# Recurrence states of four batches on the 128 partitions of a decoder layer

## The chip, the cores and the metric

The kernel runs on one core of a Trainium2 chip. The metric is the device time of one execution in microseconds. The times shown are medians of several executions; the profile is one further execution, recorded by the hardware profiler.

A core has a matrix engine (TensorE, PE in the profile, with its weight loads listed apart as PEld), a vector engine (VectorE, DVE), an engine for activation functions (ScalarE, ACT), a general engine (GpSimd, POOL) and one that issues most DMA transfers (SyncE, SP). [...]

## The reference

One decoder layer on 16 batches of 256 tokens with 256 features, all in float32. Three blocks follow each other, each with a residual and a layer normalization without gain. The change concerns the first, a gated linear recurrence:

```python
h  = x @ in_w.T + in_b                       # 256 -> 512 features
hc = conv(h, conv_w) + conv_b                # causal, 4 taps, by feature
h  = silu(hc)
xp = h @ xp_w.T + xp_b                       # 512 -> 32
a  = exp(-exp(xp[..., :16]))
b  = silu(xp[..., 16:]) * sum(h, axis=-1)
state = state * a_t + b_t                    # scan over the 256 tokens, 16 states a batch
out = states @ out_w.T + out_b               # 16 -> 256
x = layernorm(x + out)
```

The second block is an attention with 8 heads of width 128, whose queries come from x and whose keys and values come from x and from 77 context tokens. The third routes each token to two of eight experts with a limited number of places.

## The kernel before

The kernel has three stages, one after the other.

**Start** (to about 76 us). The weights are loaded on SP's queue in the order of the program. The recurrence of batches 0 and 1 is computed, and the context tokens are normalized and turned into keys' input (`kvc`) and values (`pvc`, L365).

**Loop over heads** (about 76 to 1080 us). 16 batches times 8 heads, 128 steps. Every step has on PE the products for keys and queries of its head (`pk`, `pq`), the output product of the head two steps back (`po`), the scores (`s`), and the transposes of the last head's probabilities (`pa`, `pb`). Everything else is hung into these steps: a table `steps[b, h]` lists what is issued in head h of batch b, right behind `pk` and `pq` of that head (function `at`). So while batch b runs through its heads, the next batch's recurrence and values are prepared, and the last batch's output projection (`pw`), routing and dispatch are finished.

**Experts** (from about 1080 us). The rows that were scattered to `xg` are read back, multiplied and written out.

The recurrence is done for a pair of batches, 512 tokens (`PB = 2`, `PT = 512`):

- `rec_in(pr, c)`, for each of four chunks c of 128 features: the input product `ph`, a copy with bias on ACT, the four taps on DVE, tanh on ACT, and the product that makes silu on DVE. The result is `hs`, 128 features by 4 chunks by 512 tokens, with one buffer.
- `rec_state(pr)`: the product of `hs` with `xpw`, four matmuls with 80 columns into one PSUM bank. Rows 0 to 15 of the bank are the first half of xp, rows 32 to 47 the second half, and rows 64 to 79 the sum over h (those columns of `xpw` are constants). On 16 partitions follow two exponentials and a tanh (ACT), three products (DVE) and two scans of 256 tokens (DVE), into `ysT`, whose 17th row is one and stands for the bias.
- `rec_out(b)`, for one batch: two matmuls with 17 rows (`py`), the sum with the token rows `xt`, the layer normalization, and the load of `xt` two batches on.

In the loop, for the pair that begins with batch nb = b + 1: `rec_in` in heads 4 to 7 of batch b - 1, `rec_state` in head 0 of batch b, `rec_out(nb)` in head 1, `prep_norm(nb)` in head 2, `rec_out(nb + 1)` and `prep_keys(nb)` in head 3.

PSUM tiles made by `bank()` without a tag share two banks: `px`, `py`, `ph`, `pv`, `pw`, `pt` and the router's products take turns there.

Within these lists a scheduler that builds the program may move an instruction past others on its engine; the order is fixed when the kernel is built.

Of the kernel before, what the change touches and what calls it, by code (L numbers as in the profile page):

```python
# [18 lines left out]
P = 128  # L19
B, S, D = 16, 256, 256  # L20
# [5 lines left out]
NST = 16  # L26
# [12 lines left out]
def decoder_layer(  # L39
# [44 lines left out]
    def bank(name, tag="mm", bufs=2):  # L84
        return ps.tile([P, 512], F32, tag=tag, bufs=bufs, name=name)
# [10 lines left out]
    ident = cpool.tile([P, P], F32, tag="ident", name="ident")  # L96
# [33 lines left out]
    def rsqrt(v, n, rows, name):  # L130
        r = small.tile([P, n], F32, tag="r", name=f"r{name}")
        G.tensor_tensor(r[:rows], v[:rows], nhalf[:rows, 0:n], ALU.pow)
        return r

    def layernorm(dst, src, n, rows, name):

        mv = small.tile([P, n, 2], F32, tag="mv", name=f"mv{name}")
        for i in range(n):
            st = small.tile([P, 6], F32, tag="st", name=f"st{name}_{i}")
            V.bn_stats(st[:rows], src[:rows, i, :])  # L140
            V.bn_aggr(mv[:rows, i, :], st[:rows])
        v = small.tile([P, n], F32, tag="v", name=f"v{name}")
        V.tensor_scalar(v[:rows], mv[:rows, :, 1], EPS, None, ALU.add)
        r = rsqrt(v, n, rows, name)
        for i in range(n):
            V.tensor_scalar(
                dst[:rows, i, 0:D], src[:rows, i, :], mv[:rows, i, 0:1], r[:rows, i : i + 1], ALU.subtract, ALU.mult
            )
        return mv, r
# [17 lines left out]
    aw = rec.enter_context(tc.tile_pool(name="aw", bufs=1, side="right"))  # L167
    a2 = rec.enter_context(tc.tile_pool(name="a2", bufs=2, side="right"))
# [15 lines left out]
    b2 = work.enter_context(tc.tile_pool(name="b2", bufs=2))  # L184
    b1 = work.enter_context(tc.tile_pool(name="b1", bufs=1))

    xTs, xts = {}, {}
# [6 lines left out]
    def load_x(b):  # L194
        xts[b] = aw.tile([P, 2, D], F32, tag="xt", bufs=3, name=f"xt{b}")
        nc.sync.dma_start(xts[b], x_in[b * S : (b + 1) * S, :].rearrange("(i p) d -> p i d", p=P))
# [16 lines left out]
    for t0, t1 in ((0, 1), (1, 5), (5, NCT - 1), (NCT - 1, NCT)):  # L213
        c = b2.tile([P, t1 - t0, D], F32, tag="v" if t1 - t0 == 4 else "ctx", name=f"ctx{t0}")
        rows = ctx_rows(t0)
# [2 lines left out]
        )  # L218
        ctxs += [c[:, i, :] for i in range(t1 - t0)]

    xpw = aw.tile([P, NI, 80], F32, tag="xpw", name="xpw")
    G.memset(xpw, 0.0)
    G.memset(xpw[:, :, 64:80], 0.5)
    xpw_d = xp_wT.rearrange("(c p) s -> p c s", p=P)
    nc.sync.dma_start(xpw[:, :, 0:NST], xpw_d[:, :, 0:NST])
    nc.sync.dma_start(xpw[:, :, 32 : 32 + NST], xpw_d[:, :, NST : 2 * NST])
    xpb = aw.tile([64, 1], F32, tag="xpb", name="xpb")
    G.memset(xpb, 0.0)
    nc.sync.dma_start(xpb[0:NST], xp_b[0:NST])
    nc.sync.dma_start(xpb[32 : 32 + NST], xp_b[NST : 2 * NST])  # L230
    outw = aw.tile([NST + 1, D], F32, tag="outw", name="outw")
    nc.sync.dma_start(outw[0:NST], out_wT)
    nc.sync.dma_start(outw[NST : NST + 1], out_b)
    wkv_d = wkv.rearrange("(c p) f -> p c f", p=P)
    nc.sync.dma_start(wkv_s[:, :, INNER:], wkv_d[:, :, INNER:])
    load_x(0)
# [5 lines left out]

    V.tensor_scalar(cw, cw, 0.5, None, ALU.mult)
    V.tensor_scalar(cb, cb, 0.5, None, ALU.mult)
    xpbh = aw.tile([64, 1], F32, tag="xpbh", name="xpbh")
    V.tensor_scalar(xpbh, xpb, 0.5, None, ALU.mult)

    bqs = wpool.tile([P, H], F32, tag="bqs", name="bqs")
    V.tensor_scalar(bqs, bq_s, DH**-0.5, None, ALU.mult)
# [20 lines left out]
        nc.sync.dma_start(w2_s[e], w2T[e].rearrange("(c p) d -> p c d", p=P))  # L270


    hss, yss, xs, stats = {}, {}, {}, {}

    def rec_in(pr, c):

        if c == 0:
            hss[pr] = aw.tile([P, NI, PT], F32, tag="hs", name=f"hs{pr}")
        ph = bank(f"ph{pr}_{c}")
        for k in range(DC):  # L280
            T.matmul(ph, lhsT=inw[:, k, c * P : (c + 1) * P], rhs=xTs[pr][:, k, :], start=(k == 0), stop=(k == DC - 1))  # L281
        hp = a2.tile([P, PB, KC - 1 + S], F32, tag="hp", name=f"hp{pr}_{c}")
        G.memset(hp[:, :, 0 : KC - 1], 0.0)
        A.activation(
            hp[:, :, KC - 1 :], ph.rearrange("p (b s) -> p b s", b=PB), AF.Identity, bias=inb[:, c : c + 1]
        )
        cv = a2.tile([P, PB, S], F32, tag="cv", name=f"cv{pr}_{c}")
        V.tensor_scalar(cv, hp[:, :, 0:S], cw[:, c, 0:1], cb[:, c : c + 1], ALU.mult, ALU.add)
        for k in range(1, KC):
            V.scalar_tensor_tensor(cv, hp[:, :, k : k + S], cw[:, c, k : k + 1], cv, ALU.mult, ALU.add)  # L290
        z = cv.rearrange("p b s -> p (b s)")
        th = a2.tile([P, PT], F32, tag="th", name=f"th{pr}_{c}")
        A.activation(th, z, AF.Tanh)
        V.scalar_tensor_tensor(hss[pr][:, c, :], th, 1.0, z, ALU.add, ALU.mult)

    def rec_state(pr):

        hs = hss.pop(pr)
        px = bank(f"px{pr}")
        for c in range(NI):  # L300
            T.matmul(px[0:80], lhsT=xpw[:, c, :], rhs=hs[:, c, :], start=(c == 0), stop=(c == NI - 1))  # L301
        dec = aw.tile([NST, PT], F32, tag="dec", name=f"dec{pr}")
        A.activation(dec, px[0:NST], AF.Exp, bias=xpb[0:NST])
        A.activation(dec, dec, AF.Exp, scale=-1.0)
        bs = aw.tile([NST, PT], F32, tag="bs", name=f"bs{pr}")
        A.activation(bs, px[32 : 32 + NST], AF.Tanh, bias=xpbh[32 : 32 + NST], scale=0.5)
        zb = aw.tile([NST, PT], F32, tag="zb", name=f"zb{pr}")
        V.tensor_scalar(zb, px[32 : 32 + NST], xpb[32 : 32 + NST], None, ALU.add)
        V.scalar_tensor_tensor(bs, bs, 1.0, zb, ALU.add, ALU.mult)
        V.tensor_tensor(bs, bs, px[64 : 64 + NST], ALU.mult)  # L310

        ysT = a2.tile([NST + 1, PT], F32, tag="ysT", name=f"ysT{pr}")
        G.memset(ysT, 1.0)
        for i in range(PB):
            cols = slice(i * S, (i + 1) * S)
            V.tensor_tensor_scan(ysT[0:NST, cols], dec[:, cols], bs[:, cols], 0.0, ALU.mult, ALU.add)
        yss[pr] = ysT

    def rec_out(b):

        pr, i = divmod(b, PB)
        py = bank(f"py{b}")
        for h in range(2):
            c0 = i * S + h * P
            T.matmul(py[:, h * D : (h + 1) * D], lhsT=yss[pr][:, c0 : c0 + P], rhs=outw, start=True, stop=True)
        y = b2.tile([P, 2, D], F32, tag="ya", name=f"ya{b}")
        V.tensor_tensor(
            y.rearrange("p h d -> p (h d)"),
            py,
            xts.pop(b).rearrange("p h d -> p (h d)"),  # L330
            ALU.add,
        )
        xs[b] = xpool.tile([P, 2, DX], F32, tag="xs", name=f"xs{b}")
        stats[b] = layernorm(xs[b], y, 2, P, f"a{b}")
        if b + 2 < B:
            load_x(b + 2)


    JCS = [(0, P), (P, P), (2 * P, M)]
# [322 lines left out]
    def at(b, h, f, *args):  # L662
        if 0 <= b < B:
            steps[b, h].append((f, args))
# [4 lines left out]
    for b in range(B):  # L669
        nb = b + 1  # L670
        new_pair = nb % PB == 0 and nb < B
        if b > 0:
            early = int(b == B - 1)
            at(b, 2, project, b - 1, 0)
            at(b, 3, project, b - 1, 1)
            at(b, 5 - early, turn_tokens, b - 1)
            at(b, 6 - early, score_experts, b - 1)
            at(b, 6 - early, choose, b - 1)
            at(b, 7 - early, dispatch, b - 1)
            at(b, 7, settle, b - 1)  # L680
        if new_pair:
            at(b, 0, rec_state, nb // PB)
            at(b, 1, rec_out, nb)
            at(b, 2, prep_norm, nb)
            at(b, 3, rec_out, nb + 1)
            at(b, 3, prep_keys, nb)
            for n, h in enumerate((4, 5, 6, 7)):
                at(b, h, prep_values, nb, n)
        elif nb < B:
            at(b, 0, prep_norm, nb)  # L690
            at(b, 0, prep_keys, nb)
            for n, h in enumerate((1, 4, 5, 6)):
                at(b, h, prep_values, nb, n)
            if nb + 1 < B:
                pr = (nb + 1) // PB
                at(b, 0, load_xT, pr)
                for c in range(NI):
                    at(b, 4 + c, rec_in, pr, c)

    rec_in(0, 0)  # L700
    rec_in(0, 1)
# [1 line left out]
    rec_in(0, 2)  # L703
    rec_in(0, 3)
    context(1)
    rec_state(0)
    context(2)
    context(3)
    rec_out(0)
    prep_norm(0)  # L710
    prep_keys(0)
# [21 lines left out]
    rows, xets = {}, {}  # L733
# [171 lines left out]
    for e in range(LAST + 1):  # L905
# [4 lines left out]
        y = second_product(e, it)  # L910
# [55 lines left out]
```

## Time and profile before

| what | us |
|---|---|
| median of 3 runs | 1229.26 (1229.24 to 1230.31) |
| profiled execution, its own time | 1232.08 |
| span of the profiled execution | 1230.4 |
| stage to 76 us: PE busy | 60.13 |
| 76 to 1080 us: PE busy | 995.96 of 1004 |
| 1080 to 1230 us: PE busy | 131.21 of 150 |
| px (L301): PE busy | 29.1 |
| py (L325): PE busy | 18.0 |

The mean granted clock of PE is 0.988 of full speed. A row of the profile names an engine, a line, an operation, the tile written and the tiles read, and the shape in partitions by elements. "Idle before" is the time in which the engine did nothing ahead of these instructions, and behind the arrow stands what ended it. A matmul's busy time contains time in which the next matmul already runs; so sums of busy time on PE are larger than what the matmuls take in a row.

### The profile page before, as it was taken

The numbers are of one execution on the slowest core, as the hardware profiler recorded it, in microseconds if no ns is written. First come the engines' busy times: TensorE is split into PE (matmuls) and PEld (weight loads), VectorE is DVE, ScalarE is ACT, GpSimd is POOL, SyncE is SP. The second block draws the span as 40 slices with busy tenths as digits, with TensorE's granted clock in tenths as the row PEclk, the third lists the DMA queues.
The fourth block names the chain that finished last, engine by engine and source line by source line (L and its number), as shares of the span: only waits on it lengthen the run. The fifth ranks groups of instructions, "written<-read, shape, count | busy, mean of one in ns | idle before, by whom it ended". The sixth has DMA issues, their size and how long they took to land.

```text
span 1230.4 us, 15284 instructions
## 1 busy us (share of the span) xinstructions
PE 1187.3 (96%) x5000; PEld 842.3 (68%) x5000; DVE 725.9 (59%) x2122; ACT 489.4 (40%) x1270; POOL 274.5 (22%) x500
## 2 busy tenths in 40 slices
PE   7799999999999999999999999999999999889995
PEld 3356777767776777677767776777677778756663
DVE  6535755684558555756486548564766464555654
ACT  3135434443435344534353434443543344313331
POOL 3200021122111311131111210221021112135566
PEclk9899999999999999999999999999999999999998
DMA  8730100010001100010000000000001000146762
GB/s 262 245 107 1 37 18 29 9 54 18 29 9 32 37 11 20 26 37 5 19 21 28 12 19 19 22 9 14 9 13 43 13 9 3 29 146 147 177 158 82
DMA packets 43617, 60.80 MB, mean 49 GB/s; under 512 B 7945, under 2 KB 31414, under 8 KB 43538
## 3 DMA queue, kind: packets, MB, share of 16 engines
q1 hardware_dynamic: 36674, 50.34, 12.8%
q0 software_dynamic: 6144, 9.48, 3.3%
q8 instruction: 39, 0.64, 0.2%
q14 instruction: 40, 0.33, 0.1%
q10 hardware_dynamic: 720, 0.01, 0.0%
HBM read 36.55 MB, written 30.78 MB: 55 GB/s over the span
## 4 chain that ended last, share of the span: by engine, by line
PE 82%; DVE 7%; POOL 3%; issue 3%; DMA 3%; ACT 1%; POOLq 0%; SPq 0%; DVEq 0%
PE po L484 12%; PE pk L433 10%; PE s L448 10%; PE pw L502 9%; PE pq L438 8%; PE pv L413 8%; PE ph L281 5%; PE pa L471 4%; PE pi L798 3%; PE pvc L365 3%; PE px L301 2%; PE pf L814 2%; PE pb L471 2%; PE pl L544 1%; DMA xe<-xg 1%
## 5 line engine op out<-in xcount | busy, mean ns | idle before, releaser
L450 DVE TENSOR_REDUCE nm<-s 128x2 f32<-128x666 f32 x128 | 108.4, 847 | 144.7 <-PE s L448 144.4
L484 PE MATMUL po<-ptt,v 128*128 128x256 f32 (+1 forms) x768 | 190.2, 382 | 2.2 <-DVE ptt L473 2.2
L484 PEld LDWEIGHTS po<-ptt,v 128*128 128x128 f32 (+1 forms) x768 | 144.2, 191 | 57.1 <-issue 32.7
L433 PE MATMUL pk<-kvt,wkv_s 128*128 128x333 f32 x512 | 165.1, 444 | 0.0
L448 PE MATMUL s<-kt,qt 128*128 128x333 f32 x512 | 164.4, 442 | 0.0
L492 ACT ACTIVATE ot<-po,bkv_s 128x256 f32<-128x256 f32 x128 | 60.6, 474 | 235.4 <-PE po L484 235.3
L454 ACT ACTIVATE p<-s,nm 128x333 f32<-128x333 f32 x256 | 135.1, 534 | 37.9 <-DVE nm L450 28.6
L438 PE MATMUL pq<-kvt,wq_s 128*128 128x256 f32 x512 | 131.2, 379 | 0.0
L413 PE MATMUL pv<-wkv_s,kvt 128*128 128x512 f32 x256 | 121.6, 599 | 0.0
L448 PEld LDWEIGHTS s<-kt,qt 128*128 128x128 f32 x512 | 96.5, 189 | 31.2 <-ACT qt L440 0.5
L438 PEld LDWEIGHTS pq<-kvt,wq_s 128*128 128x128 f32 x512 | 96.7, 189 | 30.5 <-issue 0.5
L474 ACT COPY ptt<-pb 77x256 f32<-77x256 f32 x128 | 47.1, 368 | 177.3 <-PE pb L471 175.9
L502 PE MATMUL pw<-wo_s,ot 128*128 128x256 f32 x512 | 117.2, 381 | 0.0
L502 PEld LDWEIGHTS pw<-wo_s,ot 128*128 128x128 f32 x512 | 97.4, 191 | 13.4 <-ACT ot L492 0.2
L433 PEld LDWEIGHTS pk<-kvt,wkv_s 128*128 128x128 f32 x512 | 87.6, 191 | 23.0
L459 DVE TENSOR_SCALAR pn<-p,rs 128x333 f32<-128x333 f32 x256 | 93.1, 397 | 4.2
L471 PEld LDWEIGHTS pa<-ident,pn 128*128 128x128 f32 x512 | 63.5, 141 | 38.7 <-DVE pn L459 11.1
L649 POOL DMA_INDIRECT xg<-xs,sidx x64 | 67.3, 1052 | 93.1 <-DVE sidx L646 78.4
L473 DVE COPY ptt<-pa 128x512 f32<-128x512 f32 x128 | 87.3, 682 | 0.9 <-PE pa L471 0.6
L513 POOL TENSOR_TENSOR xb<-xs,bo_s 128x256 f32<-128x256 f32 x32 | 21.2, 684 | 283.4 <-DVE yb L515 283.4
L471 PE MATMUL pa<-ident,pn 128*128 128x128 f32 x512 | 78.8, 274 | 5.9 <-DVE pn L459 5.9
L290 DVE SCALAR_TENSOR_TENSOR cv<-hp,cw,cv 128x512 f32<-128x512 f32 x96 | 71.4, 749 | 2.0
(167 smaller groups left out, 1596.4 us busy)
## 6 DMA issues: line engine op xcount, KB each, us to landing
v<-vc SPq DMA_DIRECT2D x16, 308.0 KB
vc<-vc SPq DMA_DIRECT2D x9, 512.0 KB
xg<-zero SPq DMA_DIRECT2D x17, 262.0 KB
xe<-xg SPq DMA_DIRECT2D x8, 524.0 KB
xT<-in_xT SPq DMA_DIRECT2D x8, 512.0 KB
xt<-in_x_in SPq DMA_DIRECT2D x16, 256.0 KB
out<-o SPq DMA_DIRECT2D x16, 256.0 KB
w<-in_w1T SPq DMA_DIRECT2D x8, 512.0 KB
```

The source lines that it names most:

```text
L290: V.scalar_tensor_tensor(cv, hp[:, :, k : k + S], cw[:, c, k : k + 1], cv, ALU.mult, ALU.add)
L413: T.matmul(pv, lhsT=kvts[b][:, k, jc * P : (jc + 1) * P], rhs=wkv_s[:, k, INNER + f0 : INNER + f0 + 512], start=(k == 0), stop=(k == DC - 1),)
L433: T.matmul(pk[:, 0:J], lhsT=wkv_s[:, k, f], rhs=kvt[:, k, :], start=(k == 0), stop=(k == DC - 1))
L438: T.matmul(pq[:, 0:S], lhsT=wq_s[:, k, f], rhs=kvt[:, k, 0:S], start=(k == 0), stop=(k == DC - 1))
L448: T.matmul(s[:, ic, 0:J], lhsT=qt[:, ic * P : (ic + 1) * P], rhs=kt, start=True, stop=True)
L450: V.tensor_reduce(nm, s[:, :, 0:J], AX.X, ALU.max, negate=True)
L454: A.activation(p[:, ic, :], s[:, ic, 0:J], AF.Exp, bias=nm[:, ic : ic + 1], accum_out=sm[:, ic : ic + 1])
L459: V.tensor_scalar(pn[:, ic, :], p[:, ic, :], rs[:, ic : ic + 1], None, ALU.mult)
L471: T.transpose(dst[0:jn, c0 : c0 + P], pn[:, ic, j0 : j0 + jn], ident)
L473: V.tensor_copy(ptt[:, 0:2, :], pt01.rearrange("p (j i) -> p j i", j=2))
L484: T.matmul(po[:, 0:S], lhsT=vs[b][0:jn, jc, h * DH : (h + 1) * DH], rhs=ptt[0:jn, jc, :], start=(jc == 0), stop=(jc == 2),)
L502: T.matmul(pws[b][:, i * D : (i + 1) * D], lhsT=ot[:, h, i * P : (i + 1) * P], rhs=wo_s[:, h, :], start=(h == 0), stop=(h == H - 1),)
```

## The change

The states of four batches lie side by side on the partitions, 32 partitions to a batch: 16 for the first half of xp, 16 for the second.

- `rec_in` adds up the four chunks of `hs` into `sums` on POOL, three additions of 128x512 for each pair. `hs` and `sums` have two buffers.
- `rec_state(first, last)` works on a group of batches: 0 and 1, 2 and 3, then 4 to 7, 8 to 11, 12 to 15. For each of four batches and each chunk there is one matmul with 32 columns and 256 tokens, which writes to the batch's 32 partitions of one bank (a column tile). Where a group has two batches, the four places hold them twice. Four more matmuls (`sg`) multiply `sums` with a constant 0.5 and so put the sum over h on all partitions. A matmul with a permutation (`perm`, 128x128) brings the second half of xp onto the partitions of the first. Exponentials, tanh, products and one scan then run on 128 partitions by 256 tokens, and `one_row` adds one to the row of each batch that stands for the bias.
- `rec_add(b)` makes the output products of two batches in turn; each has 32 rows, on partitions of its own (a row tile), and a bank of its own. It also adds `xt` and loads the next two `xt`. `rec_out(b)` keeps only the layer normalization.
- `outw` and `xpb` are loaded four times, once for each 32 partitions.
- `rec_in` of the second pair of a group comes in heads 4 to 7 of batch nb - 2, that of the first pair in heads 1, 3, 5 and 7 of batch nb - 3, where nb is the group's first batch. `rec_add` is in head 1 of every batch before a pair.

```diff
-    xpw = aw.tile([P, NI, 80], F32, tag="xpw", name="xpw")
-    G.memset(xpw, 0.0)
-    G.memset(xpw[:, :, 64:80], 0.5)
...
+    xpw = aw.tile([P, NI, 2 * NST], F32, tag="xpw", name="xpw")
+    nc.sync.dma_start(xpw, xp_wT.rearrange("(c p) s -> p c s", p=P))
+    half = aw.tile([P, 2 * NST], F32, tag="half", name="half")
+    G.memset(half, 0.5)
+    xpb = aw.tile([P, 1], F32, tag="xpb", name="xpb")
+
+    outw = aw.tile([P, D], F32, tag="outw", name="outw")
+    G.memset(outw, 0.0)
+    for g in range(0, P, 2 * NST):
+        nc.sync.dma_start(xpb[g : g + 2 * NST], xp_b)
+        nc.sync.dma_start(outw[g : g + NST], out_wT)
+        nc.sync.dma_start(outw[g + NST : g + NST + 1], out_b)
+
+    perm = aw.tile([P, P], F32, tag="perm", name="perm")
+    G.memset(perm, 0.0)
+    id4 = ident.rearrange("p (g s) -> p g s", s=2 * NST)
+    V.tensor_copy(perm.rearrange("p (g s) -> p g s", s=2 * NST)[:, :, 0:NST], id4[:, :, NST:])
+    one_row = aw.tile([P, 1], F32, tag="one_row", name="one_row")
+    V.tensor_reduce(one_row, id4[:, :, NST], AX.X, ALU.add)
...
         V.scalar_tensor_tensor(hss[pr][:, c, :], th, 1.0, z, ALU.add, ALU.mult)
+        if c > 0:
+            G.tensor_tensor(sums[pr], hss[pr][:, 0, :] if c == 1 else sums[pr], hss[pr][:, c, :], ALU.add)
...
+        px = bank(f"px{first}")
         for c in range(NI):
-            T.matmul(px[0:80], lhsT=xpw[:, c, :], rhs=hs[:, c, :], start=(c == 0), stop=(c == NI - 1))
...
+            for b, r in zip(members, rows):
+                T.matmul(
+                    px[r, 0:S],
+                    lhsT=xpw[:, c, :],
+                    rhs=hss[b // PB][:, c, tokens(b)],
+                    start=(c == 0),
+                    stop=(c == NI - 1),
+                )
+
+        sg = bank(f"sg{first}")
+        for b, r in zip(members, rows):
+            T.matmul(sg[r, 0:S], lhsT=half, rhs=sums[b // PB][:, tokens(b)], start=True, stop=True)
+        zb = aw.tile([P, S], F32, tag="zb", name=f"zb{first}")
+        V.tensor_scalar(zb, px[:, 0:S], xpb, None, ALU.add)
+        dec = aw.tile([P, S], F32, tag="dec", name=f"dec{first}")
+        A.activation(dec, zb, AF.Exp)
         A.activation(dec, dec, AF.Exp, scale=-1.0)
...
+        pp = bank(f"pp{first}")
+        T.matmul(pp[:, 0:S], lhsT=perm, rhs=zb, start=True, stop=True)
+        bs = aw.tile([P, S], F32, tag="bs", name=f"bs{first}")
+        A.activation(bs, pp[:, 0:S], AF.Tanh, scale=0.5)
+        V.scalar_tensor_tensor(bs, bs, 1.0, pp[:, 0:S], ALU.add, ALU.mult)
+        V.tensor_tensor(bs, bs, sg[:, 0:S], ALU.mult)
+        ys = a2.tile([P, S], F32, tag="ys", name=f"ys{first}")
+        V.tensor_tensor_scan(ys, dec, bs, 0.0, ALU.mult, ALU.add)
+        V.tensor_scalar(ys, ys, one_row, None, ALU.add)
+        for b, r in zip(members[0:n], rows):
+            yss[b] = ys[r, :], outw[r, :]
...
+    def rec_add(b):
+
+        pys = [bank(f"py{b + i}") for i in range(PB)]
+        for h in range(2):
+            for i in range(PB):
+                ys, w = yss[b + i]
+                T.matmul(
+                    pys[i][:, h * D : (h + 1) * D], lhsT=ys[:, h * P : (h + 1) * P], rhs=w, start=True, stop=True
+                )
         for i in range(PB):
...
+            y = b2.tile([P, 2, D], F32, tag="ya", name=f"ya{b + i}")
+            V.tensor_tensor(
+                y.rearrange("p h d -> p (h d)"), pys[i], xts.pop(b + i).rearrange("p h d -> p (h d)"), ALU.add
+            )
+            ysums[b + i] = y
+            if b + i + 2 < B:
+                load_x(b + i + 2)
...
-            at(b, 0, rec_state, nb // PB)
+            if nb == PB:
+                at(b, 0, rec_state, nb, nb + 1)
+            elif nb % 4 == 0:
+                at(b, 0, rec_state, nb, nb + 3)
+            at(b, 1, rec_add, nb)
             at(b, 1, rec_out, nb)
...
+    at(0, 0, load_xT, 1)
+    for c in range(NI):
+        at(0, 4 + c, rec_in, 1, c)
+    for nb in range(4, B, 4):
+        for i in range(2):
+            at(nb - 3 + i, 0, load_xT, nb // PB + i)
+            for c in range(NI):
+                at(nb - 3 + i, (1, 3, 5, 7)[c] if i == 0 else 4 + c, rec_in, nb // PB + i, c)
```

More of the change, by code (lines that the diff above doesn't have):

```diff
@@ L219, in decoder_layer @@
         ctxs += [c[:, i, :] for i in range(t1 - t0)]
-    xpw = aw.tile([P, NI, 80], F32, tag="xpw", name="xpw")
-    G.memset(xpw, 0.0)
-    G.memset(xpw[:, :, 64:80], 0.5)
[L224 to L233, printed above, removed]
+    xpw = aw.tile([P, NI, 2 * NST], F32, tag="xpw", name="xpw")
[15 more added lines that the diff above has]
+    V.tensor_reduce(one_row, id4[:, :, NST], AX.X, ALU.add)
     wkv_d = wkv.rearrange("(c p) f -> p c f", p=P)
@@ L244, in decoder_layer @@
     V.tensor_scalar(cb, cb, 0.5, None, ALU.mult)
-    xpbh = aw.tile([64, 1], F32, tag="xpbh", name="xpbh")
-    V.tensor_scalar(xpbh, xpb, 0.5, None, ALU.mult)
     bqs = wpool.tile([P, H], F32, tag="bqs", name="bqs")
@@ L270, in load_expert @@
         nc.sync.dma_start(w2_s[e], w2T[e].rearrange("(c p) d -> p c d", p=P))
-    hss, yss, xs, stats = {}, {}, {}, {}
+    hss, sums, yss, xs, stats = {}, {}, {}, {}, {}
     def rec_in(pr, c):
         if c == 0:
-            hss[pr] = aw.tile([P, NI, PT], F32, tag="hs", name=f"hs{pr}")
+            hss[pr] = aw.tile([P, NI, PT], F32, tag="hs", bufs=2, name=f"hs{pr}")
+            sums[pr] = aw.tile([P, PT], F32, tag="sums", bufs=2, name=f"sums{pr}")
         ph = bank(f"ph{pr}_{c}")
@@ L294, in rec_in @@
         V.scalar_tensor_tensor(hss[pr][:, c, :], th, 1.0, z, ALU.add, ALU.mult)
-    def rec_state(pr):
-        hs = hss.pop(pr)
-        px = bank(f"px{pr}")
-        for c in range(NI):
-            T.matmul(px[0:80], lhsT=xpw[:, c, :], rhs=hs[:, c, :], start=(c == 0), stop=(c == NI - 1))
-        dec = aw.tile([NST, PT], F32, tag="dec", name=f"dec{pr}")
-        A.activation(dec, px[0:NST], AF.Exp, bias=xpb[0:NST])
-        A.activation(dec, dec, AF.Exp, scale=-1.0)
[L305 to L313, printed above, removed]
-        for i in range(PB):
-            cols = slice(i * S, (i + 1) * S)
-            V.tensor_tensor_scan(ysT[0:NST, cols], dec[:, cols], bs[:, cols], 0.0, ALU.mult, ALU.add)
-        yss[pr] = ysT
@@ L319, in rec_out @@
-    def rec_out(b):
[L321 to L332, printed above, removed]
+        if c > 0:
+            G.tensor_tensor(sums[pr], hss[pr][:, 0, :] if c == 1 else sums[pr], hss[pr][:, c, :], ALU.add)
@@ new lines, in rec_state, with tokens @@
+    def rec_state(first, last):
+        n = last - first + 1
+        members = [first + g % n for g in range(4)]
+        rows = [slice(g * 2 * NST, (g + 1) * 2 * NST) for g in range(4)]
+        def tokens(b):
+            return slice(b % PB * S, (b % PB + 1) * S)
+        px = bank(f"px{first}")
+        for c in range(NI):
+            for b, r in zip(members, rows):
[13 more added lines that the diff above has]
+        A.activation(dec, zb, AF.Exp)
+        A.activation(dec, dec, AF.Exp, scale=-1.0)
+        pp = bank(f"pp{first}")
[9 more added lines that the diff above has]
+            yss[b] = ys[r, :], outw[r, :]
@@ new lines, in decoder_layer @@
+    ysums = {}
+    def rec_add(b):
[6 more added lines that the diff above has]
+                )
+        for i in range(PB):
+            y = b2.tile([P, 2, D], F32, tag="ya", name=f"ya{b + i}")
[5 more added lines that the diff above has]
+                load_x(b + i + 2)
@@ L333, in rec_out @@
+    def rec_out(b):
         xs[b] = xpool.tile([P, 2, DX], F32, tag="xs", name=f"xs{b}")
-        stats[b] = layernorm(xs[b], y, 2, P, f"a{b}")
-        if b + 2 < B:
-            load_x(b + 2)
+        stats[b] = layernorm(xs[b], ysums.pop(b), 2, P, f"a{b}")
     JCS = [(0, P), (P, P), (2 * P, M)]
@@ L693, in decoder_layer @@
                 at(b, h, prep_values, nb, n)
[L694 to L698, printed above, removed]
+    at(0, 0, load_xT, 1)
[6 more added lines that the diff above has]
+                at(nb - 3 + i, (1, 3, 5, 7)[c] if i == 0 else 4 + c, rec_in, nb // PB + i, c)
     rec_in(0, 0)
@@ L705, in decoder_layer @@
     context(1)
-    rec_state(0)
+    rec_state(0, 1)
     context(2)
     context(3)
+    rec_add(0)
     rec_out(0)
```

## The prediction

> **What bounds the kernel now.** I read the engine rows first, then the slices, then the chain that ended last, then the waits of the matmul engine.
>
> ```profile
> PE 1187.3 (96%) x5000; PEld 842.3 (68%) x5000; DVE 725.9 (59%) x2122; ACT 489.4 (40%) x1270; POOL 274.5 (22%) x500
> ...
> PE   7799999999999999999999999999999999889995
> ...
> PE 82%; DVE 7%; POOL 3%; issue 3%; DMA 3%; ACT 1%; POOLq 0%; SPq 0%; DVEq 0%
> ```
>
> PE is full from slice 3 to slice 34, and the chain runs 82% through it; no other engine passes 60%. The list of PE's waits has only these two above 3 us inside the loop over heads (76 to 1080 us) or before it, apart from the first load:
>
> ```profile
> PE pa L471 <- DVE pn L459: 5.9, 7, 3.6
> PE pt L397 <- DVE zl L385: 5.5, 1, 5.5
> ```
>
> The second is one wait at 37 us, ahead of the loop. So inside the loop the span is PE's own sum: what the change takes off PE or puts on it counts fully, and work on other engines counts only where PE comes to wait. For PE's sum, busy time misleads, because neighbouring matmuls overlap in it. The timeline gives start-to-start times instead (columns: start, busy time, engine, line, tile, rows*columns, shape, count):
>
> ```profile
> 897.37 3.60 PE L301 MATMUL px<-hs,xpw 128*80 128x512 f32 x8
> 900.80 1.46 PE L484 MATMUL po<-ptt,v 128*128 128x256 f32 x6
> ...
> 912.73 3.62 PE L502 MATMUL pw<-wo_s,ot 128*128 128x256 f32 x16
> 916.18 1.46 PE L484 MATMUL po<-ptt,v 128*128 128x256 f32 x6
> ...
> 921.24 3.62 PE L502 MATMUL pw<-wo_s,ot 128*128 128x256 f32 x16
> 924.79 1.13 PE L325 MATMUL py<-outw,ysT 17*128 17x256 f32 x4
> 925.84 0.33 PE L397 MATMUL pt<-ident,zl 128*128 128x128 f32 x1
> ```
>
> The program has four px matmuls per pair and the row counts eight: each f32 matmul is two passes, each with its own weight load. A pass over 512 columns takes (900.80-897.37)/8 = 0.429 us; over 256 columns (916.18-912.73)/16 = 0.216 us. That does not depend on the rows or columns of the array that are used: px with 80 columns and py with 17 rows cost like full ones. Going into the 17-row form costs extra: pw to py is 3.55 instead of 3.45 us (0.10), py to pt 1.05 instead of 0.86 (0.19), and the transposes behind take 0.49 instead of 0.44 (0.05, from 162.23 to 162.72 us against 165.14 to 165.58). So an excursion into a small tile and back costs about **0.35 us**.
>
> **The change, part by part, on PE.**
>
> *Removed.* px: 8 pairs x 8 passes x 0.429 = 27.5 us. py: 16 batches x 4 passes x 0.216 = 13.8. Excursions: 16 x 0.35 = 5.6. Sum 46.9 us.
>
> *Added, in passes of 256 columns.* There are five state groups (batches 0-1, 2-3, 4-7, 8-11, 12-15), each with four column tiles, filled by repeats where there are two batches. A group has 16 px and 4 sg matmuls, 40 passes, and one full matmul pp (perm), 2 passes. py keeps 64 passes, now in 8 runs of 8, two batches on two row tiles in turn. The instruction order of the changed kernel puts px and sg back to back in four groups, and splits the first into 4 and 12 px. That gives 6 excursions for the state and 8 for py.
>
> What 200 + 64 tiled passes cost depends on how many tiles run at once, and no row shows that: the trace has one tile at a time. From above it is 0.216 each. [...] I take 21, and 5 instead of 8 for a run of py.
>
> - px and sg: 5 x 21 x 0.216 = 22.7
> - pp: 10 x 0.216 = 2.2
> - py: 8 x 5 x 0.216 = 8.6
> - excursions: 14 x 0.35 = 4.9 (the row for 17 rows is nearest; column tiles may be dearer or cheaper)
>
> Sum 38.4 us, so PE is relieved of **8.5 us**. [...]
>
> **Around PE.**
>
> *pp waits for zb.* It stands behind px, sg and one pass pair of po. zb is one DVE instruction from PSUM; kvt L399 (two of 128x256 in 1.00 us) prices it at 0.50. After px, PE still has about 0.45 us of sg, a switch and 0.43 us of po. So the wait is between 0 and 0.3 us; behind it stand po, the next head's scores and all else on PE. I take 0.3 x 4 = 1.2 us.
>
> *sg waits for POOL.* Three adds of 128x512 per pair are new on POOL (xb, 128x256, takes 684 ns: an estimate of 1.4 us each, 24 of them, 33 us on an engine that is 22% busy). The last stands behind four scatter DMAs in the queue:
>
> ```profile
> 895.47 1.11 POOL L649 DMA_INDIRECT xg<-xs,sidx  x1 [0.30 <-issue]
> 896.88 1.13 POOL L649 DMA_INDIRECT xg<-xs,sidx  x1 [0.31 <-issue]
> 898.32 0.97 POOL L649 DMA_INDIRECT xg<-xs,sidx  x1 [0.30 <-issue]
> ```
>
> They end at 899.29, the last hs (DVE, from 898.30) at 899.04; with the add the sum is there at 900.7. px, starting at 897.4 and taking 16.5 pass-times, ends at 901.0: no wait. If px were four times as fast, it would end near 899.5 (held by hs), and PE would wait 1.2 us in each of four groups.
>
> *py waits for the scan.* Gone are five DVE instructions of about 0.7 us per pair on 16 partitions; there are now five per group of 128x256, 0.35 to 0.66 us. From pp to ys that is tanh, two products, scan, add: about 2.9 us with the hops, while PE has po, s, pa, pb, pk and pq, 4.6 us. Hidden; nothing is late there next, for today's py does not wait either (0.10 us is the switch).
>
> *Moved steps.* rec_in of the second pair of a quad moves by a batch, with its xT load, tanh, DVE chain and memset; it goes to heads whose number of passes it does not alter, and the total stays. Both y additions and the two xt loads behind them come at head 1; py's two banks are free once sg is read, by the same 2.9 us. Free.
>
> *Start.* SP issues 13 small loads instead of 6 ahead of wkv_s, at about 0.45 us: 3.2 us later. Its first reader in PE's order now stands behind the first px, which needs hs (17.3 us) and takes some 0.9; wkv_s had to be there by 15.8 and comes by 19.0: 0 to 0.8 us late. The first group costs PE 1.3 us more than before (it has half the batches, and is in the sum above), and the later py there is saved. I leave it at the sum, plus or minus 1.5.
>
> **Sum:** -8.5 + 1.2 = **-7.3 us**. The profiled run took 1232.08 us, of which 1230.4 are the span; it would become 1224.8. The median shown is 1229.26, 2.8 below that run; I take the difference off the median: **1222.0 us**, and 1218 to 1226 with the open terms of this case.
>
> **Rivals.**
>
> 1. *All four tiles really run together.* [...] PE -22.1, waits for POOL 4 x 1.2 and for zb 1.2: -16.1, **1213 us**.
> 2. *No overlap of f32 column tiles* (slower). The state then streams every batch by itself over 256 columns, and the sums and repeats are extra: 43.2 + 2.2 + 13.8 + 4.9 = 64.1 against 46.9, +17.2, **1246 us**; the extra passes cover the waits. For: nothing in the trace shows two tiles at once[...]. [...] It decides from the point at which 43.2/k + 2.2 + 8.6 + 4.9 + 1.2 reaches 46.9, an overlap k under 1.44.
> 3. *Weight loads come into the open at each change of tile.* [...] Nearest row: pl, 8 passes of 8 columns, from 182.57 to 183.38 us, 0.10 us each[...]. px and sg 25.4 to 33.4, py 12.1, pp 2.2, excursions 4.9: 44.6 to 52.6, and 1.2 for zb: -1.1 to +6.9, **1228 to 1236 us**. Against: in py's own run the loads are hidden.
>
> **Chances.** Pairwise overlap 0.50, all four 0.17, open weight loads 0.10, no overlap 0.23. About 0.2% (2.5 us) can be told from no change. Faster: 0.49 + 0.17 = 0.66. Within: 0.01 and two thirds of the third rival, 0.07. Slower: 0.27. For eight in ten the range reaches from most of the first rival, 1209, to 1240 with a part of the second; the likeliest case's own range is 1218 to 1226.
>
> **What would show it.** In the changed profile: start-to-start of px over a group, 16 matmuls, 32 passes: 3.5 us for pairs, 1.7 for four, 6.9 for none. py, eight passes in 1.1 us. The gap before po behind sg near 0.2 us. Waits "PE pp <- DVE zb" and "PE sg <- POOL sums": under 1.5 us in all. DVE's busy time down by about 15 us, POOL's up by about 29, with PE's waits no longer. The prediction is wrong if px starts each 0.216 us, or if sg waits for POOL in every group.

## The result and the profile after

| what | before | changed |
|---|---|---|
| median, us | 1229.78 (1229.24 to 1230.93, 4 runs) | 1219.15 (1218.34 to 1219.84, 4 runs) |
| profiled execution, us | 1232.08 | 1219.84 |
| span of it, us | 1230.4 | 1218.1 |
| granted clock of PE | 0.988 | 0.988 |

The ratio is 0.9912, with an interval of 0.9896 to 0.9927. The profiled execution became 12.2 us shorter, the median 10.6. Predicted were 7.3.

The page of the changed kernel: the row of engines, PE's slices, and the chain that ended last by engine.

```profile
PE 1169.6 (96%) x5146; PEld 836.7 (69%) x5146; DVE 719.1 (59%) x2108; ACT 480.5 (39%) x1261; POOL 304.4 (25%) x516
...
PE   6799999999999999999999999999999999889995
...
PE 83%; DVE 9%; POOL 3%; issue 2%; DMA 2%; ACT 1%; POOLq 0%; SPq 0%; DVEq 0%; ACTq 0%
```

PE is still full over the same slices and still the chain. So the gain has to be looked for in PE's own order, and the start-to-start times on PE give it: each pass is charged with the time until the next pass starts, so that waits are in it and overlap is not (`px` before is 29.1 us of busy time and 27.6 us from start to start). The program has 5146 passes instead of 5000, and the times fall all the same. By the tile written, in us, from the first pass on (at 6.3 us before, 6.4 after):

| stretch | before | changed | difference |
|---|---|---|---|
| start, to the first `pk` | 70.56 | 74.54 | +3.98 |
| batch 0's heads | 54.88 | 54.88 | 0.00 |
| batch 1's first head to the last `pw` | 948.55 | 933.05 | -15.50 |
| of this: `px` | 24.02 | 10.31 | -13.71 |
| of this: `py` | 14.79 | 7.44 | -7.35 |
| of this: `sg` and `pp` | 0 | 8.10 | +8.10 |
| of this: `pq` and `s` | 244.72 | 240.27 | -4.45 |
| of this: `pv` | 98.45 | 100.39 | +1.93 |
| behind it, to the end of the span | 150.09 | 149.24 | -0.85 |

Two things stand out. `px` with its 16 small matmuls took 2.58 us a group (10.31 / 4), waits included, where 3.5 had been reckoned for pairs of tiles; and at the same time `sg` took 6.37 us in four groups, 1.59 for the 8 passes of a group, which took 0.56 in a later experiment where nothing waited. The timeline of PE shows one group of the changed kernel (columns as before; in brackets the idle time ahead and what ended it):

```profile
521.51 1.92 PE L315 MATMUL px<-hs,xpw 128*32 128x256 f32 x28
523.83 0.41 PE L315 MATMUL px<-hs,xpw 128*32 128x256 f32 x2 [0.41 <-DVE hs L299]
523.95 0.41 PE L325 MATMUL sg<-sums,half 128*32 128x256 f32 x2
524.07 0.39 PE L315 MATMUL px<-hs,xpw 128*32 128x256 f32 x2
524.16 0.41 PE L325 MATMUL sg<-sums,half 128*32 128x256 f32 x2
525.42 0.62 PE L325 MATMUL sg<-sums,half 128*32 128x256 f32 x4 [0.85 <-POOL sums L301]
525.98 0.70 PE L514 MATMUL po<-ptt,v 128*128 128x256 f32 x2
```

28 passes are done in 1.92 us; one after the other they would take 28 x 0.216 = 6.0. Then PE waits 0.41 us for the last `hs` and 0.85 us for the sum. From the first `px` to `po` it is 525.98 - 521.51 = 4.47 us, of which only about 2.4 are work, as a later experiment shows. The start of each single pass, in us after 521.50, tells how many passes run together; the first twelve:

```
0.006 0.012 0.019 0.026 | 0.246 0.252 0.259 0.266 | 0.461 0.468 0.475 0.481
```

Four passes start within 0.02 us, and the next four 0.24 us later; from there on it is four every 0.216 us, through the 24th. A record does not name its tile; the four are taken to be of the four column tiles, since in the experiment with one batch after the other, where eight passes of one tile stand in a row, the first four start 0.22 to 0.24 us apart.

The sum on POOL came about when it was reckoned to come, 3.9 us behind the first `px` instead of 3.3. POOL's timeline, from the third scatter on:

```profile
521.63 1.12 POOL L679 DMA_INDIRECT xg<-xs,sidx  x1 [0.30 <-issue]
523.06 0.97 POOL L679 DMA_INDIRECT xg<-xs,sidx  x1 [0.30 <-DVE rs L486]
524.02 0.21 POOL L288 MEMSET hp<- 128x6 f32 x1
524.09 1.28 POOL L301 TENSOR_TENSOR sums<-sums,hs 128x512 f32<-128x512 f32 x1
```

The add starts behind the fourth scatter, 0.3 us after `hs` is done (523.78), takes 1.28 us, and PE's last `sg` starts at its end. In PE's list of waits (total, times, longest) it is now there five times, beside a new one for `hs`, one for the bank of the turned tokens (`x`, L566), and a longer one in the start:

```profile
PE pt L427 <- DVE zl L415: 6.5, 1, 6.5
...
PE sg L325 <- POOL sums L301: 4.1, 5, 0.8
...
PE px L315 <- DVE hs L299: 2.5, 4, 1.3
PE ph L286 <- DVE x L566: 1.7, 3, 0.6
```

What is missing from that list is as telling as what is in it. This line of the list before is gone:

```profile
PE po L484 <- DVE ptt L473: 2.2, 7, 0.3
```

It accounts for the 2.31 us that `pq`, which stands ahead of `po`, lost. In each of the seven waits a product of the state, on 16 partitions, stood ahead of `ptt` on DVE, as here (before):

```profile
904.78 0.68 DVE L310 TENSOR_TENSOR bs<-bs,px 16x512 f32<-16x512 f32 x1
905.50 0.69 DVE L473 COPY ptt<-pa 128x512 f32<-128x512 f32 x1
```

`s`, ahead of `pa`, lost 2.14 us, but not through the state. In six of the seven waits of `pa` before, `pn` stood behind `zl`, the layer normalization of the pair's second batch, for which DVE waited idle for POOL (before):

```profile
171.75 0.35 DVE L385 TENSOR_SCALAR zl<-xs,rlz 128x256 f32<-128x256 f32 x1 [2.83 <-POOL rlz L132]
172.02 0.69 DVE L459 TENSOR_SCALAR pn<-p,rs 128x333 f32<-128x333 f32 x2
```

The state's own instructions were over 28 us earlier there. In the changed kernel three short waits of `pa` (0.2 us each) and the long one near the end are left. The sum `ya` of that second batch now comes in head 1; whether this took the waits away, no run shows.

### The profile page after: what moved, and what is told of

It reads as the page before. It is cut to its first block, busy times and chain, and to the rows that moved or that the text cites. A ratio compares the mean times of both kernels' runs of the same rounds, so it can differ in the third digit from the quotient of the medians.

```text
span 1218.1 us, 15598 instructions
## 1 busy us (share of the span) xinstructions
PE 1169.6 (96%) x5146; PEld 836.7 (69%) x5146; DVE 719.1 (59%) x2108; ACT 480.5 (39%) x1261; POOL 304.4 (25%) x516
## 4 chain that ended last, share of the span: by engine, by line
PE 83%; DVE 9%; POOL 3%; issue 2%; DMA 2%; ACT 1%; POOLq 0%; SPq 0%; DVEq 0%; ACTq 0%
PE po L514 12%; PE pk L463 11%; PE s L478 10%; PE pw L532 9%; PE pq L468 8%; PE pv L443 8%; PE pi L837 4%; PE pa L501 4%; PE ph L286 4%; PE pf L853 3%; PE pvc L395 3%; PE pb L501 2%; DVE cv L295 2%; PE pl L574 1%; POOL xg L679 1%
```

## The experiments

A ratio is that to the kernel before on the same chip. Each experiment is built on the changed kernel, or on the one with the state in two heads where that is said.

**The changed kernel again**, on another chip, without an edit.

> The changed kernel itself, on the chip of the next three, so that they can be compared with it. 0.9912 of the kernel before, as first measured (its own interval 0.9896 to 0.9927); the start near 74.5 us up to the first head, px, sg and pp 4.6 us a group in the loop.

1218.88 us, ratio 0.9912 [0.9898, 0.9925]. The result repeats, and so do the rows of the table for `px`, `py`, `sg` and `pp`, `pq` and `s`, and `pv`, within 0.15 us each; `px`, `sg` and `pp` are 4.6 us a group. Two whole stretches do not. The start took 76.40 us instead of 74.54: from 30.7 to 37.6 us the granted clock was 0.51, and a pass of `pvc` took 0.85 us instead of 0.43. The stretch from batch 1 took 930.22 us instead of 933.05, in part because the first profile has 3.4 us at a clock of 0.50 there (from 1059.9 us) and the repeat has none. So 2 to 3 us between whole stretches of two profiles say little; the rows by tile say more.

**The order of the small matmuls.** The same matmuls, one batch after the other instead of in turn.

```diff
-        for c in range(NI):
-            for b, r in zip(members, rows):
+        for b, r in zip(members, rows):
+            for c in range(NI):
...
-        for h in range(2):
-            for i in range(PB):
+        for i in range(PB):
+            for h in range(2):
```

> Both loops are turned: px goes through the four chunks of one batch before the next batch's, and py through both halves of one batch before the other's, so neighbours in PE's list lie on the same tile. The same 264 tiled passes. Theory 'PE itself lets matmuls of another tile pass': px keeps 28 to 32 passes in about 1.9 us a group, py 8 passes in 1.1, the time stays at 1219. Theory 'only neighbours in the list overlap': a tile's 8 passes stand in a row, px takes 6 to 6.9 us a group instead of 2.4, py 1.7 instead of 0.9; of the 4.5 us a group some 1.7 cover the waits for hs and sums: +2.9 x 5 + 0.8 x 8 = +21, 1240 us.

1227.28 us, ratio 0.9960 [0.9945, 0.9974]: over half of the gain is gone with another order of the list. PE's timeline for the same group:

```profile
527.03 3.95 PE L315 MATMUL px<-hs,xpw 128*32 128x256 f32 x29
...
531.98 0.70 PE L514 MATMUL po<-ptt,v 128*128 128x256 f32 x2
```

From `px` to `po` it is now 4.95 us without a wait. The pass starts, in us after 527.00:

```
0.028 0.268 0.483 0.699 | 0.915 0.921 1.131 1.161 1.347 1.377 1.563 1.593 1.808 1.814
```

Four passes start alone, 0.22 to 0.24 us apart; with the fifth another starts 0.006 us later, and from there on it is two every 0.22 to 0.25 us. In the list eight passes of one tile stand in a row, so the second of each two is taken to be of the next tile. The time lies between the two numbers expected. `py`, with four passes of a tile in a row in this order, has the same busy time as in the order of the change (9.1 us); its added 2.56 us are a new wait of `ph`, which the scheduler put behind it in three of seven places ("PE ph L286 <- DVE ya L356: 2.3, 3, 0.8"). So the order of the passes itself costs the 3.6 us that `px` and `sg` took more from batch 1 on (20.27 instead of 16.68).

**Four and six passes of a tile in a row.** Two more orders of `px`, on the kernel with the state in two heads (e5, further below), where no wait stands in the way: two chunks of each batch in turn, and three chunks and then the fourth. The edit for three:

```diff
-        for c in range(NI):
-            for b, r in zip(members, rows):
+        for cs in ((0, 1, 2), (3,)):
+            for b, r in zip(members, rows):
+                for c in cs:
...
```

> On e5, with px in another order: two chunks of one batch, then two of the next, so that four passes of a tile stand in a row. [...]px takes 2.4 us for its 32 passes, two or three tiles at a time. [...]1.95 us or less. Theory 'only two tiles can run when a tile's passes stand in a row': 3.5 us.

> The kernel with the state split over two heads, and px in the order three chunks of each batch, then the fourth chunk of each. [...]the second, third and fourth tile start 0.43 us after each other, 32 passes take 3.0 us. [...]2.4 us or less. Rival (only neighbours in the list overlap): the fourth tile starts after 18 passes, 4 us or more.

One execution each, 1218.16 and 1218.06 us; the times are not compared, the passes are. PE's timeline of the kernel with one chunk in turn, then with two, then with three:

```profile
513.22 1.93 PE L317 MATMUL px<-hs,xpw 128*32 128x256 f32 x32
515.09 1.56 PE L530 MATMUL po<-ptt,v 128*128 128x256 f32 x6
```

```profile
513.11 1.97 PE L318 MATMUL px<-hs,xpw 128*32 128x256 f32 x32
515.01 1.56 PE L531 MATMUL po<-ptt,v 128*128 128x256 f32 x6
```

```profile
515.85 3.30 PE L318 MATMUL px<-hs,xpw 128*32 128x256 f32 x32
519.08 1.13 PE L531 MATMUL po<-ptt,v 128*128 128x256 f32 x4
```

32 passes from the first `px` to `po`: 1.87, 1.90 and 3.23 us. With two chunks the starts are, in us after the first:

```
0.000 0.013 0.027 0.040 | 0.240 0.253 0.267 0.280 | 0.456 0.469 0.483 0.496
```

Two chunks in turn cost 0.03 us. Four passes start within 0.04 us here too, again taken to be of four tiles, though four passes of a tile stand in a row in the list, so that nine of the passes that stand ahead of the fourth tile's first start later than it. Of the three times set down for two chunks, 2.4, 1.95 or less and 3.5 us, it is the second. With three chunks the starts are, in us after 515.84:

```
0.007 | 0.247 | 0.463 0.469 | 0.679 0.709 | 0.895 0.925 0.931
```

Two passes start alone, 0.24 us apart; then two within 0.006 us, two within 0.03 and three within 0.04. Six passes of a tile stand in a row here, so the second tile is taken to start with the third pass of the first, and the third tile two passes later, 0.43 us as had been set down (0.463 to 0.895). The 32 passes had been put at 3.0 us; 3.23 were measured, where 32 passes with two of a tile in a row take 1.87 instead of 8 x 0.216 = 1.73.

| passes of a tile in a row | starts | first `px` to `po`, us |
|---|---|---|
| 2 (starts of the changed kernel, time of e5) | four at once from the first on | 1.87 |
| 4 (e9) | four at once from the first on | 1.90 |
| 6 (e11) | two at once from the third on | 3.23 |
| 8 (e1) | two at once from the fifth on | 4.95, with the 8 passes of `sg` |

What lets the next tile start, the trace does not show, and three or five passes in a row were not tried.

**The fourth chunk's sum on PE.** Four more small matmuls take the place of the last addition on POOL.

```diff
-        if c > 0:
+        if 0 < c < NI - 1:
...
-            T.matmul(sg[r, 0:S], lhsT=half, rhs=sums[b // PB][:, tokens(b)], start=True, stop=True)
+            T.matmul(sg[r, 0:S], lhsT=half, rhs=sums[b // PB][:, tokens(b)], start=True, stop=False)
+        for b, r in zip(members, rows):
+            T.matmul(sg[r, 0:S], lhsT=half, rhs=hss[b // PB][:, NI - 1, tokens(b)], start=False, stop=True)
```

> POOL adds three chunks only; the fourth is added by four more sg matmuls straight from hs, on the same tiles (two more pass-times, 0.43 us a group). Theory 'sg waits for the last POOL add, which stands behind four scatter DMAs': the wait of sg (1.2 us a group in the loop, 0.8 in the start) is gone, 0.43 come back: -0.8 x 4 - 0.4 = -3.6, 1215.5 us. Rival 'pp is late anyway, because zb comes then': the wait moves to pp, within 1 us of 1219.

1216.27 us, ratio 0.9877 [0.9862, 0.9891]. From batch 1 on, `px`, `sg` and `pp` together took 16.12 us instead of 18.41, 2.3 less, and the wait of 0.8 in the start is gone too: 3.1 of the 3.6 us that were expected. (The whole stretch is 3.3 us shorter, but it was 2.8 shorter in the repeat without an edit.) The wait of `sg` is gone from the list. PE does more and the kernel is faster: the wait for POOL was worth nearly what was reckoned for it.

**The second pair's rec_in one head earlier.**

```diff
-        at(0, 4 + c, rec_in, 1, c)
+        at(0, 3 + c, rec_in, 1, c)
...
-                at(nb - 3 + i, (1, 3, 5, 7)[c] if i == 0 else 4 + c, rec_in, nb // PB + i, c)
+                at(nb - 3 + i, (1, 3, 5, 7)[c] if i == 0 else 3 + c, rec_in, nb // PB + i, c)
```

> rec_in of the second pair of each group one head earlier (heads 3 to 6 instead of 4 to 7), so that the last hs and its sum are there long before px. Theory 'px waits for hs and sg for sums, 1.7 us a group in four groups': -6.8, 1212.3 us, px and sg in 2.6 us in a row. Rival 'the DVE and POOL work now falls on the layer normalization of head 3 and delays the values and keys': less than 3 us are won, and waits of pt or pv appear.

1217.65 us, ratio 0.9902 [0.9885, 0.9918]: a miss. PE's timeline of the group:

```profile
519.99 1.93 PE L315 MATMUL px<-hs,xpw 128*32 128x256 f32 x32
521.74 0.61 PE L325 MATMUL sg<-sums,half 128*32 128x256 f32 x8
522.28 0.70 PE L514 MATMUL po<-ptt,v 128*128 128x256 f32 x2
524.39 0.70 PE L332 MATMUL pp<-zb,perm 128*128 128x256 f32 x2 [1.41 <-DVE zb L327]
```

Both waits are gone, `px` and `sg` take 2.29 us together, and the time comes back one line further down: `pp` is the next instruction that needs something of DVE. But DVE was not busy. Its timeline, and POOL's:

```profile
523.85 0.48 DVE L327 TENSOR_SCALAR zb<-px,xpb 128x256 f32<-128x256 f32 x1 [2.15 <-PE po L514]
```

```profile
522.84 0.97 POOL L679 DMA_INDIRECT xg<-xs,sidx  x1 [0.30 <-issue]
```

DVE had been idle for 2.15 us, the last `px` pass ends at 521.92 by the trace, and `zb` starts only at 523.85, where the fourth scatter on POOL ends (523.81). The view names `po` as what ended the wait, but `po` was over at 522.98. In the two other groups that run beside scatters it is the same: `zb` at 274.57 and 773.46, the scatter's end at 274.57 and 773.42. In the group at 137.87 us, where no scatter runs, `zb` starts 0.07 us behind `px` and `pp` does not wait. So what `pp` waits for is a late release of `zb`, and not the time that `zb` takes. What held it, no run here shows.

**The state in two heads.** rec_in of the second pair in heads 2 to 5; `px`, `zb` and the exponentials in head 7 of the batch before; `sg`, `pp`, products and scan in head 0.

```diff
...
-                at(b, 0, rec_state, nb, nb + 3)
+                at(b, 0, rec_scan, nb, nb + 3)
...
-                at(nb - 3 + i, (1, 3, 5, 7)[c] if i == 0 else 4 + c, rec_in, nb // PB + i, c)
+                at(nb - 3 + i, (1, 3, 5, 7)[c] if i == 0 else 2 + c, rec_in, nb // PB + i, c)
+        at(nb - 2, 7, rec_state, nb, nb + 3)
...
```

> rec_in of the second pair of each group two heads earlier (heads 2 to 5), px with zb and the exponentials in head 7, sg, pp and the scan in head 0 as before. So px, sg and pp each stand behind a head's worth of other PE work after what they need. Theory 'each of the three waits in turn, and taking one away (e2, e3) only lets the next show': all are gone, px, sg and pp cost 2.0 + 0.5 + 0.4 us and two excursions of 0.35 a group, 3.6 instead of 4.6, and what the DVE chain held up goes too: -1.0 to -1.7 in four groups, 0.996 of the changed kernel. Rival 'the DVE queue is the limit, wherever px stands': pp or py waits again, within 0.1% of the changed kernel.

1213.83 us (1211.89 to 1217.01), ratio 0.9859 [0.9844, 0.9874], the same chip having given 0.9912 for the changed kernel. The second half of the group, five microseconds behind the end of the `px` shown above for one chunk in turn:

```profile
520.35 0.64 PE L340 MATMUL sg<-sums,half 128*32 128x256 f32 x8
520.91 0.70 PE L348 MATMUL pp<-zb,perm 128*128 128x256 f32 x2
521.45 1.46 PE L530 MATMUL po<-ptt,v 128*128 128x256 f32 x6
```

No bracket is left: `px` 1.87 and `sg` 0.56 us make 2.43, against (10.31 + 6.37) / 4 = 4.17 in the changed kernel. That is 1.74 us in each of four groups, 7 us in all; `pp`, which now stands between two kinds of tile, gives 0.4 back.

**The start.** Three attempts at the 4 us: the state behind the third context tile (e4); the small loads behind `wkv_s` (e6); and, on the kernel with the state in two heads, `py` ahead of the fourth context tile and the keys behind the fifth (e10).

```diff
-    rec_state(0, 1)
     context(2)
+    rec_state(0, 1)
```

> In the start, rec_state(0, 1) is called after the third context tile instead of the second. Theory 'the start loses 4 us since px, sg and pp have no work between them and wait for hs, sums and the bank (1.3 + 0.8 + 0.9 us)': -2.5 us, 1216.6, with these waits gone. Rival 'the start is set by the layer normalization behind py, whose wait (pt for zl, 6.5 us) only grows': within 1 us of 1219.

```diff
-    for g in range(0, P, 2 * NST):
-        nc.sync.dma_start(xpb[g : g + 2 * NST], xp_b)
...
+    for g in range(0, P, 2 * NST):
+        nc.sync.dma_start(xpb[g : g + 2 * NST], xp_b)
```

> The twelve small loads of outw and xpb are issued after wkv_s and the first two xt. Theory 'the start is longer because these loads put wkv_s back by 3 us and pvc behind px': pvc comes between the ph again, the first head begins 1.5 to 2 us earlier than in the changed kernel. Rival 'the start is set by the chain px, pp, scan, layer normalization': the wait of pt for zl grows by what is won, the first head within 0.5 us.

```diff
     context(2)
-    context(3)
     rec_add(0)
     rec_out(0)
     prep_norm(0)
+    context(3)
+    context(4)
     prep_keys(0)
-    context(4)
```

> The kernel with the state split over two heads, and in the start the output products and the layer normalization of batches 0 and 1 stand behind the third context tile instead of the fourth, and the keys of batch 0 behind the fifth. Theory (the changed kernel's loss in the start is waiting: the scan's end is at 34.6 us, but 16 passes of context values stand ahead of the output products, and then PE waits 6.5 us for the layer normalization with nothing to do): the 6.5 us wait is covered by 16 context passes of 0.43 us, the start (to the first keys' product) goes from 74.4 to 68 to 69 us, the ratio to the kernel before from 0.986 to 0.981. Rival (the vector engine's chain of the context tiles sets the start): the wait comes back ahead of the context tiles' transposes, start 73 to 75 us, ratio 0.985 to 0.987.

All three missed: 1221.32 us, ratio 0.9922 [0.9909, 0.9934]; 1220.09, 0.9911 [0.9896, 0.9926]; 1214.68, 0.9871 [0.9854, 0.9887] (0.9859 without this edit). The start was 74.12 and 75.12 us in the first two. In the last it was 77.37, against 74.39 without this edit: 2.1 us of this are passes of `pvc` at a granted clock of 0.51 (from 30.4 to 37.3 us, as in the repeat), and the longest wait moved and grew:

```profile
PE pt L395 <- DVE zc L146: 8.3, 1, 8.3
```

DVE takes the context's normalization behind that of the tokens, so PE waits for it instead. What makes up the 4 us can be read from the waits of PE up to 50 us. Without the first load they add up to 8.0 us before (5.5 for `zl`, 1.9 for `kvc`, 0.6 for `hp`) and to 11.7 after: 6.5 for `zl`, and 5.2 for six short ones, most of them around the state. Three of these in the timeline of the changed kernel:

```profile
29.41 0.64 PE L315 MATMUL px<-hs,xpw 128*32 128x256 f32 x8 [1.32 <-DVE hs L299]
30.82 0.64 PE L325 MATMUL sg<-sums,half 128*32 128x256 f32 x8 [0.78 <-POOL sums L301]
...
33.02 0.96 PE L379 MATMUL pt<-ident,zc 128*128 128x128 f32 x4 [0.93 <-DVE bs L335]
```

A further 0.9 us is in the first eight passes of `ph`, 6.28 instead of 5.42 us; that is a matter of the run, for in the repeat they took 5.56. The sum on PE took away 0.8 of the waits. In the repeat the clock made the start 1.9 us longer still, so the 4 us are those of one pair of profiles. Whether another order of the start avoids the rest stays open.

## Why the prediction was right and wrong

The direction was right, the size nearly: -10.6 us measured, -7.3 predicted. The mechanism was not, and that the total came so near is luck: errors of 2 to 10 us stood against each other. `px` and `sg` were priced at 22.7 us and are about 12 of work (5 x 2.43), and a relief of 4.5 us ahead of `po` and `pa` was put at nothing; waits of 4.6 us from batch 1 on, 3.7 us more of waits in the start, and 1.9 us by the moved steps took much of that back.

**The step that failed** is the 21 pass-times for the 40 passes of a group, for which the tiles have to run in pairs. The row was right (two passes per matmul); that tiles overlap in pairs was the author's assumption, and no row of before showed it. These runs show something else: four passes start within 0.02 us, taken to be the first of four tiles, though second passes stand between them in the list. With two chunks in turn whole matmuls stand between them: four passes have started within 0.04 us, and the first tile's second matmul, which is second in the list, starts at 0.46 us, if a tile's passes keep their order. 32 px passes took 1.87 us where nothing waited, not 3.5. Of the three numbers set down for `px` it was the one of the rival "all four tiles really run together", 1.7. That rival's -22.1 takes 10 pass-times for the 40 passes (10.8 + 2.2 + 6.9 + 4.9 = 24.8 us against 46.9), which was an assumption too. With one batch after the other `px` and `sg` took 4.95 us, near the 4.9 of 21 pass-times and a switch; two passes do run at a time there, but with eight passes of a tile in a row.

**No wait of `sg` for POOL** failed as a consequence; that `sg` waits in every group is one of the prediction's own two signs of being wrong. The working had the other branch too, 1.2 us in each of four groups if px were four times as fast, "held by hs". Measured: 4.1 us for `sg` in five groups, and with it 2.5 us for `hs` in four, which had no price. The fourth chunk on PE brought back 3.1 us, the state in two heads 5.05 us of the median on one chip (1218.88 to 1213.83). The rival's gain of 16.1 us already holds 6.0 us of waits, more than the 4.6 measured from batch 1 on; most of what is missing to it lies in the start, which became 4.0 us longer.

**`pp` waits for `zb`, 0.3 us in each of four groups**, did not show in the changed kernel, where `sg`'s wait stood ahead of it. With the earlier rec_in it was 1.3 to 1.8 us in three groups and nothing in the fourth. The working counted the time that `zb` takes, which was right (0.48 us); the late release of `zb` had no place in it, and its cause stays open.

**py**: 1.06 us per run of eight, 7.44 / 7, switches included, as the sum for two row tiles at a time has it (4 x 0.216 and 0.19). Five pass-times had been taken; it is four.

**DVE's relief at nothing** was wrong. "Gone are five DVE instructions of about 0.7 us per pair" was reckoned only for `py`. One of them had stood ahead of `ptt` in each pair: with it went 2.31 us ahead of `po`. The 2.14 us ahead of `pa` went with the waits of `pn` behind `zl`, another change in DVE's list, which was not priced either. The view that showed the first was there before, a wait of 2.2 us in seven pieces, one for each pair; no piece was above 0.3 us.

**Moved steps, "free"**: not quite. The stretch of `pv` grew by 1.93 us, and 1.7 of it are three waits of `ph` for a bank that the turned tokens hold, since the first pair's rec_in is now in heads 1, 3, 5 and 7 (argued from the order, not tried).

**Start, "at the sum, plus or minus 1.5"**: the sum had 1.3 us more, it became 4.0. The work of the group was priced, its waits for `hs`, POOL and the bank of `pp` were not. The late loads, priced at 0 to 0.8, were not the cause: moving them changed nothing.

DVE's busy time fell by 6.8 us instead of 15, POOL's rose by 29.9, as said (29). The state's own DVE instructions did fall by 15.5; the last section has the rest.

Rivals two and three are ruled out by the same pass starts: in the order of the change four passes start every 0.216 us, so no tile ran alone, and `px` and `sg` took about 12 us of work where the third rival had 25.4 to 33.4, the author's estimate of weight loads in the open.

## What to carry to other kernels

Give small matmuls to their tiles in turn, few in a row for each: here four passes in a row took as long as two (1.90 and 1.87 us), six or eight cost a factor of 1.7 to 2.2 (3.23 and about 16.35 / 4 = 4.09 us against 1.87). When PE gets faster through a stretch, price the next two or three instructions that need another engine, each as if the one ahead had stopped waiting: `hs`, then the sum, then `zb` came up one behind the other, the last for a cause that is not known, and only putting other work between the halves removed them all. And a list of many short waits, one for each repeat of the part that is changed, belongs in the sum like one long wait.

## What was not expected of the hardware

The order in which passes start. With two and with four passes of a tile in a row, four start within 0.02 and 0.04 us; with six in a row two passes start alone at first, with eight four do.

Some instructions of DVE took longer while POOL made an addition of `sums`. The router's `eq` takes 0.17 us, but 0.83 in the six of 16 first uses that meet an addition. In the changed kernel, DVE's timeline and then POOL's:

```profile
193.21 0.83 DVE L601 TENSOR_TENSOR eq<-lg,m 128x16 f32<-128x16 f32 x1
194.08 0.18 DVE L603 TENSOR_TENSOR key<-eq,rev 128x16 f32<-128x16 f32 x1
```

```profile
192.73 1.28 POOL L301 TENSOR_TENSOR sums<-sums,hs 128x512 f32<-128x512 f32 x1 [1.75 <-DVE hs L299]
```

The add ends at 194.01, `eq` at 194.04. `zl` took 0.98 us instead of 0.35 in three cases and `carry` 0.85 instead of 0.17 in three; `m` and `lg` (0.17) and the copies of `v` (0.69) beside the same additions took no longer. The six `eq` and the three `carry` start 0.46 to 0.54 us behind the start of an addition and end 0.03 us behind its end, the three `zl` 0.15 us behind it; the other ten first uses of `eq` and the other 13 of `carry` took 0.17 to 0.18 us. The additions are new in the changed kernel, and in the one before no `eq` and no `carry` took over 0.18 us. What holds the slow ones, no run shows. `eq`, `zl` and `carry` together add 8.7 us to DVE's time; how much of it reaches PE was not tried.
